# Token diffusion with earlier queries and squares, four single-bank PSUM tiles, two score tiles, and three more pauses in the work beside it

## Chip, cores and metric

The kernel runs on one core of one Trainium2 chip. The metric is the time on the device in microseconds. A profile of one execution accompanies the times; durations and waits come from it. The engines are TensorE (PE, with its weight loads PEld), VectorE (DVE), ScalarE (ACT), GpSimd (POOL) and SyncE (SP), which here issues most DMA transfers.

## What is computed

The reference chains four blocks on a tensor x of 8 sequences of 512 tokens and 256 channels: differential attention, two layers of local attention with a gated feed-forward part, a block of token and channel diffusion, and a mixture of 8 experts of which each token takes 2. Each block has the form x = x + layernorm(block(layernorm(x))). The change lies in the third block and in the beginning of the fourth:

```python
# token diffusion, 16 heads of 16 channels; queries and keys are the same projection
qk = (x @ Wqk).reshape(b, n, H, dh).transpose(0, 2, 1, 3)
v  = (x @ Wv).reshape(b, n, H, dh).transpose(0, 2, 1, 3)
dot = einsum('bhnd,bhmd->bhnm', qk, qk)
q2 = sum(qk * qk, axis=-1)
logits = (2.0 * dot - q2[..., :, None] - q2[..., None, :]) / sqrt(dh) * tau
out = einsum('bhnm,bhmd->bhnd', softmax(logits), v)
return out @ Wo            # reshaped back to (b, n, d)
# channel diffusion: the same between channels, 8 groups of 32
# x = x + token(ln(x)) * gamma1 ; x = x + channel(ln(x)) * gamma2
# experts, gate only:
gates = softmax(xf @ gate_w); topw, topi = top_k(gates, 2)
```

## The kernel before

All of x stays in SBUF as fp32. The kernel goes through the blocks one after the other. The third block (`diffusion`, which calls `tokens`) takes the eight sequences in turn; the experts follow when all are gated.

**Steps and slots.** `tokens` handles a sequence in four steps of four heads each; step n is sequence n // 4, heads 4 (n % 4) and up. Each step has four slots, k = 0 to 3, one for each tile of 128 tokens. The loop over `s` in `tokens` walks over all slots: `scores(n, k)` makes a group of four score products, one for each head in its own quarter of TensorE's rows, into two PSUM tiles `tsa` of two heads each, and ACT turns each into exponentials `te` (L1007, L1011). `sums` multiplies the exponentials with the values into one accumulator `tpo` for the step (L1020), which ACT copies to `toc`; `divide` transposes it (`tpt`), and DVE divides by the sum of the exponentials (L1039, L1040: `trec`, `to`). 

**Queries and squares.** `queries(n + 1)` projects the next step's queries and keys (`tqk`). ACT copies the product to `tkT` (L955), DVE squares it (`tsq`, L956), POOL scales it to `tqT` (L957). `squares(n + 1)` sums the squares with a product (`tq`) and adds them to `tkT` and `tqT` on DVE (L965, L968). Only then can the scores of step n + 1 begin. In this kernel queries stand in slot k = 1 and squares in slot k = 2. (All `tau` are positive in the inputs, so the branch `known` is the one that runs.)

**Work beside it.** Two queues of generators, `between` and `ahead`, are advanced from the loop: a call runs one generator as far as its next `yield`. `between` is called twice in every slot. It holds `finish(b)` of the sequence before, 17 calls, and then `gate(b)`, 10 calls. `finish` transposes the output (`toT`, copied by ACT and DVE in turn), multiplies it by Wo (`pp`), normalises (`th`), does the channel diffusion (`cqk`, `cpd`, `cpr`, `cpw`, `cpv`, and a `pp` with the folded weight `wvc`), and adds the result to x on POOL (L889). `gate` takes moments of x, normalises it into `xf`, stores it, transposes it, makes the gate's product `pg`, ranks the eight experts for each token on DVE and POOL (`ahead`, `same`, `rank`, `sel`, `run`), makes the positions with two products into `ppos`, and scatters the rows of `xf` to DRAM with eight indirect DMAs from POOL (L1228). `xf` has a single buffer, so the next gate's first write to it (L1169, on POOL) waits until those have landed. `ahead` holds `prepare(b + 1)`: norms, transposes and values of the next sequence.

**PSUM.** There are eight banks. Pool `t_big` has three tiles of two banks for scores; pool `t_ps` has two tiles of one bank for everything else: `tqk`, `tq`, `tpo`, `tpt`, and all the products of finish, gate and prepare.

**Order.** The order of the instructions on each engine is set when the program is built: a planner takes the instructions in the order of the text, with its own costs, and lets those marked `high_priority(offset=HOLD)` go ahead. Groups marked `keep_in_program_order` stay together. On the chip each engine runs its own list in order, and a semaphore wait holds all that stands behind it.

Of the kernel before, what the change touches and what calls it, by code (L numbers as in the profile page):

```python
# [14 lines left out]
PSUM = bass.MemoryType.PSUM  # L15
# [101 lines left out]
class Net:  # L117
# [690 lines left out]
    def diffusion(self, nb, rest):  # L808

        nc, g = self.nc, self.dw
        later = lambda n, b, **k: rest.enter_context(self.tc.tile_pool(name=n, bufs=b, side="right", **k))
        wk, small, ps = later("t_wk", 1), later("t_small", 3), later("t_ps", 2, space=PSUM)
        tiles = lambda x: [x[:, t, :] for t in range(NT)]
        last = (wk.tile([P, NT, D], F32, name="tyl", tag="tyl"), wk.tile([P, NT, TH, 16], F32, name="tol", tag="tol"))

        def finish(b, y, o):

            oT = wk.tile([P, DC, S], F32, name="toT", tag="chT")  # L820
            self.turned(ps, o.rearrange("p t h e -> p t (h e)"), oT)
            yield

            def add(t0, pp):
                nc.vector.tensor_add(y[:, t0:t0 + 2, :], y[:, t0:t0 + 2, :], pp)

            for t0 in range(0, NT, 2):
                self.project(ps, lambda t: [oT[:, c, self.tok(t)] for c in range(DC)], [g["o"][:, c, :] for c in range(DC)], add, [t0])
                yield

            made = self.moments(small, tiles(y))
            yield
            h = wk.tile([P, NT, D], F32, name="th", tag="th")
            self.normed(tiles(y), tiles(h), *made)
            yield
            hT = wk.tile([P, DC, S], F32, name="chT", tag="chT")
            self.turned(ps, h, hT, g["g2"], g["b2"])
            yield
            qk = wk.tile([P, NT, D], F32, name="cqk", tag="cqk", bufs=1)
            for t0 in range(0, NT, 2):  # L840
                self.project(ps, lambda t: [hT[:, c, self.tok(t)] for c in range(DC)], [g["cqk"][:, c, :] for c in range(DC)],
                             lambda t0, pp: self.copy(qk[:, t0:t0 + 2, :], pp), [t0])
                yield
            pd = ps.tile([P, DC, P], F32, name="cpd", tag="ps")
            for i in range(DC):
                self.mm(pd[:, i, :], [(qk[:, t, self.tok(i)], qk[:, t, self.tok(i)]) for t in range(NT)])
            dot = small.tile([P, DC, P], F32, name="dot", tag="dot", bufs=1)
            nc.vector.tensor_copy(dot, pd)
            dg = small.tile([P, DC, P], F32, name="dg", tag="dg", bufs=1)
            nc.vector.tensor_mul(dg, dot, self.ident.unsqueeze(1).to_broadcast([P, DC, P]))  # L850
            yield
            pr = ps.tile([P, DC, P], F32, name="cpr", tag="ps")
            self.mm(pr, [(self.const[:, C_ONE:C_ONE + P], dg)])

            nc.vector.scalar_tensor_tensor(dot, dot, 2.0, pr, ALU.mult, ALU.subtract)
            for i in range(DC):
                nc.vector.scalar_tensor_tensor(dot[:, i, :], dot[:, i, :], g["ct"][:, i:i + 1],
                                               self.const[:, C_BLK:C_BLK + P], ALU.mult, ALU.add)
            nm = small.tile([P, DC], F32, name="cnm", tag="cnm")
            nc.vector.tensor_reduce(nm, dot, AX.X, ALU.max, negate=True)  # L860
            rs = small.tile([P, DC], F32, name="crs", tag="crs")
            for i in range(DC):
                nc.scalar.activation(dot[:, i, :], dot[:, i, :], AF.Exp, bias=nm[:, i:i + 1], accum_out=rs[:, i:i + 1])
            nc.vector.reciprocal(rs, rs)
            nc.vector.tensor_mul(dot, dot, rs.unsqueeze(2).to_broadcast([P, DC, P]))
            yield
            yield

            pw = ps.tile([P, DC, D], F32, name="cpw", tag="ps")
            for i in range(DC):  # L870
                self.mm(pw[:, i, :], [(dot[:, i, :], g["co"][:, i, :])])
            wc = wk.tile([P, DC, D], F32, name="wc", tag="wc", bufs=1)
            self.copy(wc, pw)
            yield
            pv = ps.tile([P, DC, D], F32, name="cpv", tag="ps")
            for i in range(DC):
                self.mm(pv[:, i, :], [(g["cv"][:, c, self.tok(i)], wc[:, c, :]) for c in range(DC)])
            wv = wk.tile([P, DC, D], F32, name="wvc", tag="wvc", bufs=1)
            self.copy(wv, pv)
            yield  # L880
            yield
            for t0 in range(0, NT, 2):
                if t0:
                    yield
                self.project(ps, lambda t: [hT[:, c, self.tok(t)] for c in range(DC)], [wv[:, c, :] for c in range(DC)], add, [t0])
            made = self.moments(small, tiles(y))
            yield
            self.normed(tiles(y), tiles(y), *made)
            nc.gpsimd.tensor_add(self.xb(b), self.xb(b), y)  # L889
            self.between.add(self.gate(b, wk, small, ps))  # L890

        self.logs = True
        flag = nc.values_load(self.flag, min_val=0, max_val=1)
        with self.tc.If(flag > 0) as known:
            self.tokens(nb, True, wk, small, ps, finish, last)
        with known.Else():
            self.tokens(nb, False, wk, small, ps, finish, last)
        self.joint()
        self.between = Between()
        self.between.add(finish(nb - 1, *last))  # L900

    def joint(self):
# [3 lines left out]
    def tokens(self, nb, known, wk, small, ps, finish, last):  # L906
# [4 lines left out]

        with ExitStack() as ctx:
            pool = lambda n, b, **k: ctx.enter_context(self.tc.tile_pool(name=n, bufs=b, **k))
            step, big = pool("t_step", 2), pool("t_big", 3, space=PSUM)
            nc, g = self.nc, self.dw
            state, qk, es, pos, outs = {}, {}, {}, {}, {}
            group = lambda i: slice(32 * i, 32 * i + 32)
# [42 lines left out]
            def squares(n):  # L960
                qT, kT, sq = qk[n]
                pq = ps.tile([P, S], F32, name="tq2", tag="ps")
                self.mm(pq, [(self.const[:, C_G:C_G + P], sq)])
                with self.tc.high_priority(offset=HOLD if known else 0):
                    nc.vector.scalar_tensor_tensor(kT, pq, self.const[:, C_K17:C_K17 + 1], kT, ALU.mult, ALU.add)  # L965
                    if known:
                        r = n % 4
                        nc.vector.scalar_tensor_tensor(qT, pq, g["sq"][:, r:r + 1], qT, ALU.mult, ALU.add)  # L968
# [76 lines left out]
            total = 4 * nb  # L1045
# [6 lines left out]
            for s in range(4 * (total + 1) if known else 0):  # L1052
                n, k = divmod(s, 4)
                if n < total:
                    scores(n, k)
                if k == 0 and n:
                    sums(n - 1, 2)
                    sums(n - 1, 3)
                if k == 1 and n + 1 < total:
                    queries(n + 1)  # L1060
                if k == 1 and n:
                    divide(n - 1)
                if k == 2 and n + 1 < total:
                    squares(n + 1)
                if k == 3 and n < total:
                    sums(n, 0)
                    sums(n, 1)
                if k == 1 and n % 4 == 0 and n < total:
                    if n // 4 + 1 < nb:
                        ahead.add(prepare(n // 4 + 1))  # L1070
                    if n:
                        b = n // 4 - 1
                        between.add(finish(b, state[b][0], outs.pop(("o", b))))
                between()
                if k % 2:
                    ahead()
                between()
            for s in range(0 if known else 8 * (total + 2)):
                n, j = divmod(s, 8)
# [77 lines left out]
    def gate(self, b, wk, small, ps):  # L1157
# [33 lines left out]
        nc.vector.tensor_tensor(same, theirs, mine, ALU.is_equal)  # L1191
        nc.gpsimd.tensor_mul(same, same, tie.unsqueeze(1).to_broadcast([P, NT, NE, NE]))
        nc.gpsimd.tensor_add(ahead, ahead, same)
        rank = small.tile([P, NT, NE], F32, name="rank", tag="rank")
        nc.vector.tensor_reduce(rank, ahead, AX.X, ALU.add)
        yield
# [7 lines left out]
            nc.vector.memset(run[:, 0, :], 0.0)  # L1204
        for t in range(NT):
            nc.vector.tensor_add(run[:, t + 1, :], run[:, t, :], sel[:, t, :])
        pp = ps.tile([P, NT, NE], F32, name="ppos", tag="ps")
        flat = lambda x: x.rearrange("p t e -> p (t e)")
        self.mm(flat(pp), [(row(C_TRI, P), flat(sel)), (row(C_ONE, P), flat(run[:, 0:NT, :]))])
# [261 lines left out]
```

## Time and profile before

| | us |
|---|---|
| median of 3 runs | 4023.95 (4018.45 to 4028.95) |
| the profiled execution | 4028.8 |
| its span | 4027.1 |
| PE busy | 3577.5 |
| DVE busy | 2220.8 |
| ACT busy | 1828.2 |
| POOL busy | 1612.7 |
| score products of token diffusion, first to last start | 2778.5 to 3443.9 |

The span is the time from the first to the last recorded instruction. An engine's busy time is a share of that span, and neither tells by itself what the end waits for. A timeline row gives an instruction's start, its duration, and in brackets how long its engine stood idle before it and whose end released it. A granted clock of 1.00 is TensorE's full speed.

### The profile page before, as it was taken

Reading aid. Unit: us, or ns where it says so; the run is one execution under the profiler, and the core shown is the slowest. Engines: PE = TensorE matmul, PEld = TensorE weight load, DVE = VectorE, ACT = ScalarE, POOL = GpSimd, SP = SyncE. Lnnn points to the kernel's source line nnn. Section 1 sums busy time; section 2 is a strip of 40 time slices with the busy share of each in tenths; the row PEclk is TensorE's granted clock in tenths of the full one; section 3 lists DMA queues with packets and bytes.
Section 4 is the critical chain, followed back from the end, with each engine's and each line's share of the span. In section 5 each row is a group of like instructions: output and inputs, shape, how many; then the busy total and the mean of one; then the engine's idle time right before and its main releaser. Section 6 shows DMA issues by size and latency. Waiting matters only on the chain. (4 is left out here: it accounts for less than half of the span.)

```text
span 4027.1 us, 53567 instructions
## 1 busy us (share of the span) xinstructions
PE 3577.5 (89%) x20002; PEld 1911.0 (47%) x20002; DVE 2220.8 (55%) x4380; ACT 1828.2 (45%) x3639; POOL 1612.7 (40%) x1459
## 2 busy tenths in 40 slices
PE   8999999999878999999999999977888888578883
PEld 3343434443335555555555555643444444355562
DVE  6677767776636666665555555533444433344444
ACT  3555555555524444444444444424555444223333
POOL 3666666666644333333333333311111111143344
PEclk8999999999979999999999999988999999789996
DMA  9200000000000000000000000000000000421123
GB/s 349 98 1 6 6 6 1 6 6 6 6 32 1 5 4 3 3 23 4 9 29 9 9 9 9 9 16 22 16 17 16 16 16 16 145 66 53 52 89 104
DMA packets 92878, 130.46 MB, mean 32 GB/s; under 512 B 23040, under 2 KB 71238, under 8 KB 92614
## 3 DMA queue, kind: packets, MB, share of 16 engines
q1 hardware_dynamic: 86086, 109.10, 8.3%
q0 software_dynamic: 6528, 17.87, 1.2%
q8 instruction: 162, 2.65, 0.3%
q14 instruction: 102, 0.84, 0.1%
HBM read 57.58 MB, written 65.18 MB: 30 GB/s over the span
## 5 line engine op out<-in xcount | busy, mean ns | idle before, releaser
L359 ACT ACTIVATE e<-sa 128x1024 f32<-128x1024 f32 (+3 forms) x512 | 359.2, 702 | 347.8 <-PE sa L352 345.3
L380 POOL TENSOR_TENSOR e<-e,e 128x1536 f32<-128x1536 f32 (+2 forms) x192 | 451.6, 2352 | 98.7 <-PE po L375 88.7
L352 PE MATMUL sa<-qT,kT 32*128 32x512 f32 (+3 forms) x2048 | 436.6, 503 | 8.5 <-ACT e L359 8.1
L342 PE MATMUL sc<-kT,qT 32*128 32x128 f32 (+3 forms) x2048 | 427.5, 499 | 8.7 <-DVE spread L356 5.2
L356 DVE TENSOR_REDUCE spread<-sc 128x2 f32<-128x256 f32 (+3 forms) x512 | 422.1, 825 | 15.3
L633 ACT ACTIVATE lp<-lp,lnm 128x256 f32<-128x256 f32 (+1 forms) x512 | 240.0, 470 | 255.8 <-DVE lnm L625 161.1
L200 PE MATMUL lpa<-ghT,lw 128*128 128x512 f32 (+1 forms) x768 | 341.5, 599 | 14.7 <-ACT ghT L546 14.7
L637 POOL TENSOR_TENSOR lp<-lp,lrs 128x1024 f32<-128x1024 f32 x64 | 121.1, 1893 | 550.5 <-DVE lrs L634 550.5
L355 DVE TENSOR_TENSOR sc<-sc,const 128x256 f32<-128x256 f32 x512 | 218.5, 427 | 166.6 <-PE sa L352 142.6
L342 PEld LDWEIGHTS sc<-kT,qT 32*128 32x128 f32 x2048 | 161.9, 190 | 287.6 <-issue 126.1
L1011 ACT ACTIVATE te<-tsa 128x1024 f32<-128x1024 f32 x256 | 250.4, 1023 | 71.1 <-PE tsa L1007 59.9
L200 PE MATMUL lqk<-qkv,lhT 128*128 128x512 f32 x512 | 246.0, 619 | 2.3 <-DVE qk L584 1.6
L585 POOL TENSOR_TENSOR qk<-qk,over 128x1024 f32<-128x1024 f32 x64 | 151.2, 2363 | 216.1 <-DVE qk L584 216.1
L200 PEld LDWEIGHTS lpa<-ghT,lw 128*128 128x128 f32 (+1 forms) x768 | 133.0, 178 | 207.8 <-issue 167.6
L362 POOL TENSOR_SCALAR_AFFINE_SELECT e<-e 128x512 f32<-128x512 f32 x256 | 160.3, 639 | 172.6 <-ACT e L359 172.5
L1324 ACT ACTIVATE ehT<-eht,enorm 128x128 f32<-128x128 f32 x288 | 108.0, 457 | 232.0 <-PE eht L1320 232.0
L375 PE MATMUL po<-e,v 128*32 128x512 f32 (+3 forms) x2048 | 189.9, 454 | 4.0 <-POOL e L362 3.6
L200 PE MATMUL lpp<-lw,u 128*128 128x256 f32 (+1 forms) x768 | 193.2, 396 | 0.0
L622 DVE TENSOR_TENSOR lp<-lsc,const 128x768 f32<-128x768 f32 (+1 forms) x128 | 138.6, 1083 | 91.6 <-PE lsc L619 91.5
L619 PE MATMUL lsc<-lkT,lqT 64*128 64x256 f32 (+1 forms) x1024 | 158.1, 388 | 27.6 <-DVE qk L584 27.6
L352 PEld LDWEIGHTS sa<-qT,kT 32*128 32x128 f32 x2048 | 161.1, 191 | 42.9 <-ACT e L359 26.7
L200 PE MATMUL py<-ew,ehT 128*128 x576 | 146.6, 399 | 37.5 <-ACT ehT L1324 19.4
(277 smaller groups left out, 6865.8 us busy)
## 6 DMA issues: line engine op xcount, KB each, us to landing
xrows<-zero SPq DMA_DIRECT2D x66, 514.0 KB
ex<-xrows SPq DMA_DIRECT2D x72, 128.5 KB
ew<-in_L_ffn_w_dram SPq DMA_DIRECT2D x16, 512.0 KB
egot<-yrows SPq DMA_DIRECT2D x16, 512.0 KB
x<-in_L_attn_X_dram SPq DMA_DIRECT2D x8, 512.0 KB
saved<-x SPq DMA_DIRECT2D x8, 512.0 KB
lx<-saved SPq DMA_DIRECT2D x8, 512.0 KB
xf<-xf SPq DMA_DIRECT2D x8, 512.0 KB
```

The costliest lines, as they stand in the source:

```text
L200: self.nc.tensor.matmul(out, lhsT=l, rhs=r, start=i == 0, stop=i == len(pairs) - 1)
L342: nc.tensor.matmul(sc[:, i, :w], lhsT=qT[g, self.tok(t)], rhs=kT[g, :w], start=True, stop=True)
L352: nc.tensor.matmul(sa[:, i, :S - k * P], lhsT=kT[g, self.tok(k)], rhs=qT[g, k * P:], start=True, stop=True)
L355: nc.vector.tensor_add(sc[:, :, w - P:w], sc[:, :, w - P:w], own)
L356: nc.vector.tensor_reduce(self.spread[n % 2][:, t, g0:g0 + 2, 0 if n % 2 else 16], sc[:, :, :w], AX.X, ALU.max, negate=True)
L359: nc.scalar.activation(x[:, h0:h0 + 2, :], sa[:, :, :S - k * P], AF.Exp, scale=0.25)
L362: nc.gpsimd.affine_select(x[:, :, :P], x[:, :, :P], [[0, 4], [1, P]], ALU.is_ge, 0.0, base=0, channel_multiplier=-1)
L375: nc.tensor.matmul(pos[n][group(g), k * P:], lhsT=seqs[b][1][:, k, 4 * r + g, :], rhs=x[:, g, :], start=k == 0, stop=k == 2)
L380: nc.gpsimd.tensor_add(y, y, es.pop((n, k)))
L619: nc.tensor.matmul(sc[:, i, c0:c0 + m * P], lhsT=qT[r, h, self.tok(t)], rhs=kT[r, h, k0 * P:(k0 + m) * P], start=True, stop=True)
L633: nc.scalar.activation(x, x, AF.Exp, bias=nm[:, i, k:k + 1], accum_out=rs[:, i, k:k + 1])
L1011: nc.scalar.activation(e[:, 2 * i:2 * i + 2, :], sa[i], AF.Exp)
```

## The change

Four things change, all in the third block and in the gate:

- `queries` of the next step move from slot k = 1 to slot k = 0, and `squares` from slot k = 2 to slot k = 1.
- Pool `t_ps` gets four banks instead of two.
- Pool `t_big` gets two score tiles instead of three. All eight banks are in use as before.
- Three more `yield`s are put in: one in `finish` between the add to x and the moment at which the gate joins the queue, one in `gate` ahead of the rank, one ahead of the product for the positions.

```diff
-        wk, small, ps = later("t_wk", 1), later("t_small", 3), later("t_ps", 2, space=PSUM)
+        wk, small, ps = later("t_wk", 1), later("t_small", 3), later("t_ps", 4, space=PSUM)
...
             nc.gpsimd.tensor_add(self.xb(b), self.xb(b), y)
+            yield
             self.between.add(self.gate(b, wk, small, ps))
...
-            step, big = pool("t_step", 2), pool("t_big", 3, space=PSUM)
+            step, big = pool("t_step", 2), pool("t_big", 2, space=PSUM)
...
-                if k == 1 and n + 1 < total:
+                if k == 0 and n + 1 < total:
                     queries(n + 1)
                 if k == 1 and n:
                     divide(n - 1)
-                if k == 2 and n + 1 < total:
+                if k == 1 and n + 1 < total:
                     squares(n + 1)
...
         nc.gpsimd.tensor_add(ahead, ahead, same)
+        yield
         rank = small.tile([P, NT, NE], F32, name="rank", tag="rank")
...
             nc.vector.tensor_add(run[:, t + 1, :], run[:, t, :], sel[:, t, :])
+        yield
         pp = ps.tile([P, NT, NE], F32, name="ppos", tag="ps")
```

The line numbers in the text are those of the kernel before; in the changed kernel lines behind the first `yield` move down by one, behind the second by two and behind the third by three.

## The prediction, made before the changed kernel was run

> **What bounds the kernel now.** I read the page, then busy time and clock by stretch, then TensorE's own timeline, then who ended its idle time. The page gives the whole:
>
> ```profile
> PE 3577.5 (89%) x20002; PEld 1911.0 (47%) x20002; DVE 2220.8 (55%) x4380; ACT 1828.2 (45%) x3639; POOL 1612.7 (40%) x1459
> PEclk8999999999979999999999999988999999789996
> ```
>
> TensorE (PE) is the busiest engine, and the edits lie only in token diffusion, 2778 to 3450 us of the span. Busy time and granted clock, first of three long stretches of that stage, then of one sequence cut at TensorE's holes:
>
> ```profile
> 2778.00:2858.00 80.00, 78.09 (x469) 31.88 (x468) 23.64 (x57) 54.50 (x68) 7.08 (x6) 1.00 0.00 1
> 2858.00:3396.00 538.00, 474.32 (x2653) 231.12 (x2654) 221.05 (x679) 274.07 (x393) 97.61 (x103) 0.93 0.05 18
> 3149.53:3153.47 3.94, 0.00 (x1) 0.03 (x1) 2.26 (x7) 0.28 (x1) 2.40 (x2) 0.82 0.00 0
> 3153.47:3158.50 5.03, 5.03 (x14) 1.71 (x14) 3.32 (x17) 4.50 (x8) 0.00 (x0) 0.50 0.21 73
> 3169.49:3172.33 2.84, 0.00 (x0) 0.03 (x1) 1.19 (x7) 1.94 (x2) 1.36 (x2) 1.00 0.00 0
> 3172.33:3179.66 7.33, 7.18 (x20) 3.31 (x20) 3.28 (x17) 0.69 (x1) 3.92 (x5) 0.53 0.15 54
> ```
>
> Columns: length, then PE, weight loads, DVE, ACT, POOL, the clock, DMA. The first sequence has no finish or gate of another beside it and nearly no holes (78.09 of 80). Then six sequences take 538 us, 89.7 each (cpd product to cpd product, 2857.86 to 3395.86). Two holes recur in each, 3.94 and 2.84 us, and after each the clock is half (0.50, 0.53) for 5.03 and 7.33 us: 2.5 + 3.4 = 5.9 us lost besides. Who ended TensorE's holes, 2862 to 3450:
>
> ```profile
> PE pt L192 <- DVE to L1040: 23.6, 6, 3.9
> PE ppos L200 <- DVE two L1217: 14.2, 5, 2.8
> PE tsa L1007 <- DVE tqT L968: 12.0, 7, 1.7
> PE cpw L200 <- DVE dot L865: 5.3, 7, 0.8
> PE pt L192 <- ACT chT L196: 2.9, 5, 0.6
> ```
>
> So a sequence loses 3.94 + 2.84 + 1.72 + 0.75, about 1.1 in small ones (0.26, 0.23, 0.58), and 5.9 of clock: 16.2 of 89.7 us. What is left is work: a group of four score products takes 1.07 us start to start, two value groups (tpo) 1.86, tqk 1.75, tq 0.96, tpt 0.53, a pp of eight products 3.6, eight transposes 1.05.
>
> **What the change removes, from the order in which the changed program is built.**
> - The 3.94: a transpose (pt) waits for the bank that tpt holds until DVE's `to`, and DVE stands in order behind bn_stats of x, which waits 2.35 us for POOL's add (L889). Four banks free it, and the gate's moments now come after tpt's readers. -3.94.
> - The 2.84: ppos waits for the ranking on DVE and POOL (3168.4 to 3172.3). With the new yields there stand, between pg and ppos, scores 1.07, tpt 0.53, tq 0.96, four pp 1.83 and scores 1.07: 5.5 us against a chain of some 5 (tsq 0.7 now in it). -2.84.
> - The 1.72: scores wait for tqT (L968), as tq came one slot earlier than they. Two slots lie between now. -1.72.
> - The half clock behind the first two: -5.9.
> Sum -14.4 us a sequence. Joined transposes give some -0.4.
>
> **What it adds.** The built order is fixed per engine, so I walked it with the durations above.
>
> A. *The scatter.* In before, three scatter DMAs, POOL's tqT (L957), then five; the tqT after those came late enough to wait for nothing:
>
> ```profile
> 3178.57 0.88 POOL L957 TENSOR_SCALAR tqT<-tkT,dsa,dsb 128x512 f32<-128x512 f32 x1
> 3179.62 1.02 POOL L1228 DMA_INDIRECT xrows<-xf,slots  x1 [0.17 <-issue]
> ...
> 3184.73 0.96 POOL L1228 DMA_INDIRECT xrows<-xf,slots  x1 [0.30 <-issue]
> 3187.66 0.54 POOL L1169 TENSOR_SCALAR xf<-const 128x4 f32<-128x4 f32 x2 [1.97 <-DMA xrows<-xf,slots]
> 3192.41 1.26 POOL L957 TENSOR_SCALAR tqT<-tkT,dsa,dsb 128x512 f32<-128x512 f32 x1 [4.22 <-ACT tkT L955]
> ```
>
> After the change all eight DMAs stand together, then the next gate's token column (it waits until they have landed), then tqT of the next sequence's second step, whose queries come earlier. From ppos: slots 3.1 us, first issue 3.4, eight issues at 1.26 (five took 6.07) to 13.25, landing 2 to 2.5, column 0.54, tqT 1.0: 17 us. DVE then does tqT's square (L968, 0.74) and only behind it the copy of toT (0.69), which pp of Wo needs: 18.7. TensorE gets there after ppos 1.04, scores 2.0, tpo 1.86, scores 1.07, tpo 1.86, tqk 1.75, scores 1.07, tpt 0.53, tq 1.0, pt 1.05, scores 1.07: 14.3. It stands 4.4 us, and the half clock after it costs 2.7 (between 2.5 and 3.4). +7.1.
>
> B. *Two tiles of scores.* A group's first pair waits for the first exponential of the group before, its second pair for the second. ACT reads in order:
>
> ```profile
> 3153.97 0.30 ACT L156 ACTIVATE rs<-mv,const 128x4 f32<-128x4 f32 x1 [4.16 <-DVE mv L173]
> 3154.30 0.21 ACT L157 ACTIVATE rs<-rs 128x4 f32<-128x4 f32 x1
> 3154.41 1.00 ACT L1011 ACTIVATE te<-tsa 128x1024 f32<-128x1024 f32 x1
> ```
>
> There an exponential stands behind the gate's rs, that one behind bn_stats of x and POOL's add. It still does. From the end of pp of Wvc: ty 1.8, rs, normalised by 4.6, add to 7.0, four bn_stats and aggregates to 8.9, rs to 9.5, exponential to 10.5. Now the last score group of that step needs it, and stands directly behind the third: TensorE arrives at 5.1, waits 1.4 for the first exponential, works 0.86, waits 3.1, works 0.86. That and 0.45 in the group before is 5.7 us more than the work, and 2.7 of half clock. +8.4.
>
> C. Other split groups: beside ppos 0.9, around cpr 1.4 (the exponentials of one group, 1.94 us, against 0.54 of cpr between). +2.3.
>
> D. th: both rs now stand together on ACT behind both sets of moments, and transposes wait about 2.0 where 1.07 was lost. +1.0 (0 to 2).
>
> Added 18.8 against 14.8 removed: +4.0 us for each of seven sequences, +28. In the first sequence, where before has next to no holes, third and fourth score group are adjacent in each of four steps; a pair at 2.2 and one at 3.2 us after the group's start instead of 1.07 ends about 1.5 later: +6. The gate's extra yields use 30 of 32 calls of the queue, so nothing spills into the next sequence; the tail's waits (3445 to 3520) are its own dependency chain, 0. No instruction is added.
>
> Sum: profiled span 4027.1 + 34 = 4061; the execution took 4028.8, the median of the runs is 4023.95, so **4058 us**.
>
> **A rule against the row.** Half clock is the term I know least. Row: half clock followed a hole of 2.84 us as well as one of 3.94. The Trainium skill, "TensorE: Matmul & The Clock Gate", section "HAM oscillation — how this bites in real kernels", has only idle gaps longer than about 3.4 us matter. By the rule B's holes (1.4, 3.1) would cost no clock, and the 2.84 removed should not have: 7 x 2.7 = 19 us less, 4039. By the row, 4058. I keep the row, measured in this stage, and put the rule's value in the range.
>
> **Rivals.**
> 1. *Faster, 0.20.* A isn't there. Place: pp of Wo, once a sequence. Price: 7.1 x 7 = 50 us, so 4008; with the clock rule also 3989. It decides when POOL's chain from ppos to tqT is shorter than TensorE's way there, 14.3 us instead of 18.7: if under about 0.5 us of A's 7.1 is left, the sum is below -12. For it: both holes named by the profile do go. Against: eight issues at 1.26 and a landing of 2 us are read from before.
> 2. *The exponentials pace everything, 0.17.* ACT was busy 46 us of 89; with every group tied to the one before, each late copy on ACT (toc, tkT) also holds TensorE. Split groups at some twelve more places cost 0.86 each: 10 us x 8, 4140. Against: most groups have 2.5 us or more of other products between.
> 3. *Banks and clock pay each other off, 0.12.* Half clock in A and B is smaller (38 us less): 4020, no change.
>
> **How the numbers follow.** My case 0.51. 0.3% of this time, 12 us, is about what can be told from no change. Its own range is 4025 to 4090 (4 us a sequence either way). The range for 8 in 10 reaches into rivals 1 and 2: 3988 to 4112. My case has 0.03 of its chance within 0.3%: faster 0.20, same 0.15, slower 0.65.
>
> **What would show it.** Right: no hole at pt behind `to`, none over 1 us at ppos; a hole of 3 to 5 us before pp of Wo, released by DVE toT, and POOL's tqT ending about 17 us after ppos; a hole of about 3 us inside a score group, released by ACT te; a sequence of 93 to 95 us; first sequence about 6 us longer. Wrong: sequences under 89 us, clock above 0.95 in this stage, or POOL's tqT free before the squares.

## The result, and the profile after

The changed kernel takes 4048.33 us (median, 4038.52 to 4057.56) against 4021.39 us before (4016.55 to 4032.38), measured side by side: a ratio of 1.006, interval 1.0043 to 1.0078. That is slower by 27 us; 4058 was predicted. The profiled execution of the changed kernel took 4039.01 us, one of its fastest, and that of the kernel before, at 4028.8, lies in the upper half of its runs. So the two traces differ by 10 us only, and what follows explains the stage in which the edits lie, not each of the 27.

The page of the changed kernel, TensorE's share and its granted clock:

```profile
PE 3601.6 (89%) x20002; PEld 1914.0 (47%) x20002; DVE 2222.8 (55%) x4380; ACT 1830.5 (45%) x3639; POOL 1612.4 (40%) x1459
PEclk8999999999979999999999999988989999789996
```

No instruction was added, and TensorE is busy for 24 us longer. Busy time by stretch, with the columns of the prediction (length, then PE, weight loads, DVE, ACT, POOL, the clock, DMA), for the first sequence and the six behind it, cut at the first cpd product of each:

```profile
2778.00:2862.94 84.94, 79.60 (x452) 31.88 (x453) 22.36 (x53) 53.42 (x66) 6.74 (x6) 1.00 0.00 1
2862.94:3411.87 548.93, 494.14 (x2653) 232.96 (x2652) 222.56 (x679) 274.44 (x393) 96.72 (x102) 0.92 0.05 18
```

Six sequences take 548.9 us, 91.5 each, where they took 538.0 (89.7). TensorE idles less (54.8 us for 63.7) and is busy longer (494.1 for 474.3). Who ended its idle time, 2862 to 3450 us of the changed kernel (total, times, longest):

```profile
PE tsa L1008 <- ACT te L1012: 32.4, 27, 3.5
PE pp L200 <- DVE toT L149: 17.5, 6, 4.7
PE cpw L200 <- DVE dot L865: 5.3, 7, 0.8
PE pt L192 <- DVE th L181: 4.9, 6, 0.9
```

All three rows that led this list before (pt behind `to`, ppos, scores behind tqT) are gone. Two new ones stand for them: scores behind an exponential (the prediction's B) and the product with Wo behind `toT` (its A). TensorE's timeline in the first of the six sequences has both, in the bracket of the row:

```profile
2891.30 1.13 PE L1008 MATMUL tsa<-tqT,tkT 32*128 32x512 f32 x4 [1.13 <-ACT te L1012]
2895.18 2.08 PE L1008 MATMUL tsa<-tqT,tkT 32*128 32x512 f32 x4 [2.76 <-ACT te L1012]
...
2935.45 6.32 PE L200 MATMUL pp<-dwo,toT 128*128 128x256 f32 x14 [4.71 <-DVE toT L149]
```

For B, ScalarE's timeline of the same sequence shows who is late:

```profile
2893.68 0.30 ACT L156 ACTIVATE rs<-mv,const 128x4 f32<-128x4 f32 x1 [2.44 <-DVE mv L173]
2894.01 0.20 ACT L157 ACTIVATE rs<-rs 128x4 f32<-128x4 f32 x1
2894.12 1.01 ACT L1012 ACTIVATE te<-tsa 128x1024 f32<-128x1024 f32 x1
```

The exponential has its scores, but stands behind the gate's `rs`, for which ScalarE waits 2.44 us. For A, GpSimd's timeline and then VectorE's (ppos was at 2915.60):

```profile
2928.12 0.96 POOL L1231 DMA_INDIRECT xrows<-xf,slots  x1 [0.30 <-issue]
2931.95 0.53 POOL L1170 TENSOR_SCALAR xf<-const 128x4 f32<-128x4 f32 x2 [2.87 <-DMA xrows<-xf,slots]
2932.59 0.77 POOL L958 TENSOR_SCALAR tqT<-tkT,dsa,dsb 128x512 f32<-128x512 f32 x1
```

```profile
2933.39 0.75 DVE L966 SCALAR_TENSOR_TENSOR tkT<-tq,const,tkT 128x512 f32<-128x512 f32 x1 [5.43 <-POOL tqT L958]
2934.06 0.74 DVE L969 SCALAR_TENSOR_TENSOR tqT<-tq,dsq,tqT 128x512 f32<-128x512 f32 x1
2934.72 0.68 DVE L149 COPY toT<-pt 128x512 f32<-128x512 f32 x1
```

The last of eight scatter DMAs, the token column that waits for their landing, tqT at last (it ends 17.8 us after ppos), VectorE's two squares behind 5.43 us of waiting, and `toT` behind those.

**A ledger of the six sequences.** From the records of TensorE and of its clock over the six sequences of a trace I added up the time without PE work ("idle"), the clock that was not granted (1 less the clock, times the length: "half clock"), the part of it that fell on busy time, and the rest of PE's busy time ("work at full clock", in which score products that stand in pairs instead of fours are included with their longer time):

| us in six sequences | length | idle | half clock | of it on busy time | work at full clock |
|---|---|---|---|---|---|
| before | 538.0 | 63.7 | 35.8 | 31.3 | 443.0 |
| after | 548.9 | 54.8 | 42.7 | 36.8 | 457.4 |

So the change won 8.9 us of holes and gave back 5.4 of clock and 14.4 of work. The holes removed were larger than those made; the loss is where no row of waits shows it. Taken by tile, the work has grown at the score products: 125.0 us at full clock where they took 105.3, while all other products together take 5.3 less.

### The profile page after: what moved, and what is told of

It reads as the page before. It is cut to its first block, busy times and chain, and to the rows that moved or that the text cites. A ratio compares the mean times of both kernels' runs of the same rounds, so it can differ in the third digit from the quotient of the medians.

```text
span 4037.3 us, 53548 instructions
## 1 busy us (share of the span) xinstructions
PE 3601.6 (89%) x20002; PEld 1914.0 (47%) x20002; DVE 2222.8 (55%) x4380; ACT 1830.5 (45%) x3639; POOL 1612.4 (40%) x1459
## 5 line engine op out<-in xcount | busy, mean ns | idle before, releaser
L1008 PE MATMUL tsa<-tqT,tkT 32*128 32x512 f32 x1024 | 187.0, 660 | 38.1 <-ACT te L1012 38.0
L958 POOL TENSOR_SCALAR tqT<-tkT,dsa,dsb 128x512 f32<-128x512 f32 x32 | 34.6, 1081 | 459.2 <-ACT tkT L956 458.6
```

What stands on the lines that cost most here:

```text
L1008: m = nc.tensor.matmul(sa[i // 2][:, i % 2, :], lhsT=kT[q, self.tok(k)], rhs=qT[q, :], start=True, stop=True)
```

## Experiments

Each is compared with runs of the kernel before on the same chip. "Period" is the mean of the six sequences in its own trace. The kernel before has 89.7, the changed one 91.5.

| run | what it is | median us | ratio to before | interval | period us |
|---|---|---|---|---|---|
| e1_psum | before + bank split | 4055.32 | 1.0058 | 1.0037 to 1.0078 | 92.8 |
| e1_queries | before + moved queries and squares | 4025.62 | 0.9988 | 0.9979 to 0.9997 | 88.7 |
| e1_yields | before + three pauses | 4030.35 | 1.0003 | 0.9992 to 1.0013 | 91.0 |
| e1_qy | after, bank split undone | 4059.68 | 1.0066 | 1.0042 to 1.009 | 95.5 |
| e2_qact | after, tqT on ScalarE | 4014.66 | 0.9974 | 0.9963 to 0.9986 | 85.6 |
| e2_rspool | after, gate's rs on GpSimd | 4016.28 | 0.9982 | 0.9971 to 0.9993 | 87.0 |
| e2_both | after, with both | 3990.88 | 0.9914 | 0.9891 to 0.9936 | 82.1 |
| e2_before_qact | before, tqT on ScalarE | 4022.82 | 0.9996 | 0.9985 to 1.0008 | 89.7 |
| e3_sums | e2_both, first value product earlier | 4012.01 | 0.9958 | 0.9944 to 0.9973 | 86.4 |
| e3_three_tiles | e2_qact, bank split undone | 4018.05 | 0.9973 | 0.9964 to 0.9982 | 89.5 |
| e3_no_pauses | e2_both without the pauses | 4008.71 | 0.9947 | 0.9931 to 0.9964 | 85.6 |
| e4_no_queries | e2_both without the moved queries | 4049.47 | 1.0053 | 1.0039 to 1.0068 | 91.4 |

The period is not the whole of a run: the first and the last sequence change too, and what stands behind the seventh cpd product takes 620 to 638 us in the fourteen traces. In e1_yields, for one, the six sequences are 8 us longer than before and the stretch from the seventh to the eighth cpd product is 7 shorter (70.8 for 77.7).

**The parts alone.** Each of the first three has only its own lines of the change's diff; e1_qy has all but the two lines of the pools:

```diff
-        wk, small, ps = later("t_wk", 1), later("t_small", 3), later("t_ps", 4, space=PSUM)
+        wk, small, ps = later("t_wk", 1), later("t_small", 3), later("t_ps", 2, space=PSUM)
...
-            step, big = pool("t_step", 2), pool("t_big", 2, space=PSUM)
+            step, big = pool("t_step", 2), pool("t_big", 3, space=PSUM)
```

> Only the PSUM split of the change (four small banks, two score tiles); queries, squares and pauses as before. Theory (the sum of the prediction): the hole at pt behind DVE to (3.94 us) goes, with 2.5 of half clock; the hole at ppos (2.84) stays; hole A stays away, as POOL's scatter order is that of before; the hole inside a score group (B, 1.1 + 2.8 us in the changed kernel) is there, with its half clock, and the first sequence is about 5 us longer. Net about +1 to +3 us a sequence: 4030 to 4050. Rival (the two score tiles cost nothing for themselves, the loss is in the queries and the scatter): the 6.4 us a sequence are won, about 3980, and the first sequence is no longer than before.

> Only the move of queries and squares by one slot; banks, score tiles and pauses as before. Theory: the wait of scores for tqT (1.7 us a sequence) goes, the holes at pt (3.9) and ppos (2.8) stay, no hole inside a score group; 4010 to 4025. Rival (the earlier queries by themselves put tqT behind the gate's work on POOL and make hole A): slower, 4030 to 4050, with a wait at pp of Wo behind DVE toT.

> Only the three pauses; banks, score tiles, queries and squares as before. Theory: the hole at ppos (2.8 us) goes with its half clock (3.4), and the gate's moments leave DVE before to, so that the hole at pt shrinks as well; nothing of A or B is there: 3970 to 4000. Rival (the pauses only move the wait, for what runs on TensorE's spare time anyway): within 12 us of before, 4010 to 4034.

> The whole change without the PSUM split (two small banks, three score tiles). Theory: B and the split score groups are gone, the first sequence is as before, hole A (pp of Wo behind DVE toT, mean 2.9 us in the changed kernel) is still there: 5 to 8 us a sequence less than the changed kernel, 3985 to 4010. Rival (half clock comes whatever the holes are, so that the score tiles are not what costs): within 12 us of the changed kernel, 4036 to 4060.

The bank split alone costs 0.58%, as much as the whole change, a little above the range given; its first waits, 2862 to 3450:

```profile
PE tq L200 <- DVE tsq L956: 21.0, 7, 3.2
PE tsa L1007 <- DVE tqT L968: 19.6, 6, 3.6
PE tsa L1007 <- ACT te L1011: 12.6, 20, 1.5
PE ppos L200 <- DVE two L1217: 5.0, 5, 1.0
```

The hole at pt behind `to` is gone, but not its cause. VectorE still stands behind the moments of x; now `tsq` is caught there too, and the squares' product waits 3 us for it. The 2.8 us hole of B did not come (the longest wait for an exponential is 1.5), and tqT waits for the scatter here as well: at 3013.6 it stands behind all eight DMAs. So the mechanisms that I expected of this kernel were the wrong ones, though the time was nearly right.

The moved queries alone are 0.12% faster, below what can be told from no change, as expected. What I did not expect is the row for pt behind `to`: 6.6 us in all where it was 23.6. With the queries a slot earlier VectorE does tqk's and tpt's work ahead of the moments. The holes shrink from 63.7 to 45.8 us in six sequences, but half clock grows from 35.8 to 39.2 and work by 9.

The three pauses alone change nothing (the rival). The hole at ppos is away, without a row; in its place stand smaller ones, and the hole at pt was not touched, against what I expected:

```profile
PE pt L192 <- DVE to L1041: 23.7, 6, 3.9
PE tsa L1008 <- DVE tqT L969: 12.0, 7, 1.7
PE tpo L1021 <- DVE tqT L969: 5.7, 5, 1.1
```

Without the bank split the change is as slow (1.0066), where 3985 to 4010 was expected. The hole of the scatter became larger, since with two small banks the transposes of `to`, ahead of the product with Wo, already wait for the bank that the squares hold until VectorE has used tqT. First rows of its waits:

```profile
PE pt L192 <- DVE tqT L969: 36.8, 12, 6.3
PE pp L200 <- DVE to L1041: 13.4, 6, 2.2
```

So "the bank split is the loss and the rest is a gain" is wrong. Nor does A belong to one of the edits. GpSimd's timeline of e1_queries, behind the eighth scatter DMA:

```profile
2920.81 0.54 POOL L1169 TENSOR_SCALAR xf<-const 128x4 f32<-128x4 f32 x2 [2.40 <-DMA xrows<-xf,slots]
2921.45 1.11 POOL L957 TENSOR_SCALAR tqT<-tkT,dsa,dsb 128x512 f32<-128x512 f32 x1
```

In e1_psum (3013.6), e1_yields (2929.95) and e1_qy (2930.42), too, a tqT stands behind all eight, where in the kernel before only three were ahead of it. What differs is which product of TensorE needs that tqT, and how soon: scores in e1_psum, transposes for up to 6.3 us in e1_qy, the product with Wo in the whole change. B needs the two score tiles and the new order together, since neither e1_psum nor e1_qy has such a hole. So there are no two halves of this change of which one could be kept, and the next experiments take A and B away and leave the change whole.

**A and B taken away.** e2_qact scales tqT on ScalarE; e2_rspool computes the gate's `rs` on GpSimd, which the kernel does elsewhere; e2_both has both; e2_before_qact is the first edit in the kernel before:

```diff
-                    nc.gpsimd.tensor_scalar(qT, kT, g["sa"][:, r:r + 1], g["sb"][:, r:r + 1], ALU.mult, ALU.add)
+                    nc.scalar.activation(qT, kT, AF.Identity, bias=g["sb"][:, r:r + 1], scale=g["sa"][:, r:r + 1])
...
+        logs, self.logs = self.logs, False
         made = self.moments(small, tiles(self.xb(b)))
+        self.logs = logs
```

> The changed kernel with tqT scaled by ACT instead of POOL (32 instructions of about 0.7 us move to ACT, which has room), so that the scatter DMAs on POOL no longer stand before it. Theory (A is POOL's scatter ahead of tqT): the holes at pp of Wo behind DVE toT (17.5 us in six sequences) and the half clock beside them go: 15 to 40 us less than the changed kernel, 4008 to 4033. Rival (what holds toT is DVE's own queue, or the half clock comes anyway): within 12 us of the changed kernel.

> The changed kernel with the gate's rs (4 values a partition) computed on POOL instead of ACT, so that no exponential stands behind it. Theory (B is the exponential behind rs): the holes of 2.76 us inside a score group go, with the half clock behind them: 15 to 40 us less than the changed kernel, 4008 to 4033; A stays as it is or grows by what TensorE comes earlier. Rival (two score tiles make it wait for the exponential whatever stands ahead on ACT): within 12 us of the changed kernel, the same holes released by ACT te.

> The changed kernel with both: tqT on ACT and the gate's rs on POOL. Theory: A and B are all that the change adds beside split score groups, so their sum is won: 35 to 75 us less than the changed kernel, 3973 to 4013, faster than before. Rival (the two hide each other, as a hole later in the same stretch takes up what the first leaves): no more than the better of the two alone.

> The kernel before with tqT on ACT, as the control: there tqT waits for no scatter that TensorE feels. Theory: only the part of the wait of scores for tqT (1.7 us a sequence) that POOL's 0.9 to 1.3 us made is won: 4010 to 4030, no change that counts. Rival (POOL's tqT is what paces all versions): 20 us or more faster than before.

Each repair turns the slower kernel into one faster than before: 1.006 to 0.9974 (34 us by the medians) and to 0.9982 (32 us). Together they give 0.9914, 57 us less than the changed kernel, most of 34 + 32. The waits, 2862 to 3450, first of e2_qact:

```profile
PE tsa L1008 <- ACT te L1012: 33.9, 28, 2.8
PE cpw L200 <- DVE dot L865: 5.3, 7, 0.8
PE pt L192 <- DVE th L181: 5.1, 6, 0.9
```

of e2_rspool:

```profile
PE tsa L1008 <- ACT te L1012: 15.9, 27, 1.1
PE pp L200 <- DVE toT L149: 12.8, 6, 3.1
```

of e2_both, with its six sequences below:

```profile
PE tsa L1008 <- ACT te L1012: 15.6, 25, 1.1
PE cpw L200 <- DVE dot L865: 8.6, 8, 3.3
```

```profile
2870.38:3362.83 492.45, 468.52 (x2653) 225.62 (x2652) 220.93 (x679) 289.70 (x405) 79.58 (x90) 0.98 0.06 20
```

Each edit removes its own row and leaves the other's: `toT` falls from 17.5 to 0.3 us with tqT on ScalarE (a row of 0.3 is left), the longest wait for an exponential from 3.5 to 1.1 with `rs` off ScalarE. A and B are thus shown as causes. In the kernel before, tqT on ScalarE is worth nothing, so ScalarE is not simply the better place for it. The same control was not run for `rs`; in the trace of the kernel before TensorE waits for exponentials for 0.3 us in all between 2862 and 3450, so little could be won there by this path. The ledger:

| us in six sequences | length | idle | half clock | of it on busy time | work at full clock |
|---|---|---|---|---|---|
| e2_qact | 513.4 | 39.2 | 22.2 | 17.9 | 456.3 |
| e2_rspool | 522.1 | 37.0 | 25.6 | 25.5 | 459.5 |
| e2_both | 492.4 | 23.9 | 10.2 | 10.2 | 458.3 |

Taking A away won 15.6 us of holes and 18.9 of clock: more than half of its price was clock. The work stays at 456 to 460 in all three, 13 to 16 above before, and again at the score products (125 to 127 us at full clock, 105.3 before). That part of the change's cost is neither A nor B. The prediction has split score groups (C) for it; the next runs bear on that.

**Can C go too, and is each part needed?** e3_sums is e2_both with one value product a slot earlier, so that it stands between two score groups:

```diff
-                if k == 3 and n < total:
+                if k == 2 and n < total:
                     sums(n, 0)
+                if k == 3 and n < total:
                     sums(n, 1)
```

e3_three_tiles is e2_qact with two small banks and three score tiles (`rs` stays on ScalarE). e3_no_pauses and e4_no_queries are e2_both without the three `yield`s, and with queries and squares in slots 1 and 2.

> The changed kernel with tqT on ACT, the gate's rs on POOL, and besides the first value products of a step (sums of tile 0) in slot 2 instead of slot 3, so that four groups of eight value products stand apart between score groups instead of two pairs. In the built order 28 of the 128 score groups of this stage then become 3 that have less than 0.87 us of other work ahead of them. Theory (C, groups split by the exponential of the group before, each 0.5 to 1.1 us of hole and 0.86 of half-filled array): 25 groups by 1.0 to 1.6 us are won, 25 to 40 us less than with both: 3950 to 3966. Rival (the split groups only wait for what TensorE waits for later anyway): within 12 us of both, 3979 to 4003.

> The moved queries, the three pauses and tqT on ACT, with the banks of the kernel before (two small, three score tiles). Theory (with two small banks a transpose waits for the bank that tq or tpt holds, whatever makes tqT): the holes of 5.8 us behind tqT at the scatter go, those behind to and thT stay, 3990 to 4015, so the four banks are worth something beside B. Rival (the three score tiles are worth as much as the four banks): 3975 to 3990, as good as the changed kernel with both repairs.

> The changed kernel with both repairs (tqT on ACT, the gate's rs on POOL) but without the three pauses. Theory: the hole at ppos (about 1.0 to 2.8 us with its half clock of 2.5) comes back in six or seven sequences, 10 to 35 us more than with both: 4000 to 4025. Rival (the pauses do nothing once A and B are gone): within 12 us of both, 3979 to 4003.

> The changed kernel with both repairs (tqT on ACT, the gate's rs on POOL) but with queries and squares in the slots of the kernel before. Theory (the sum of the prediction: the move of queries takes away the wait of scores for tqT, 1.72 us a sequence, with up to 3.4 of clock): that wait is back, 10 to 35 us more than with both: 4000 to 4025. Rival (a later square stands between score groups that are adjacent in the changed kernel, 12 short gaps instead of 28 among the 128 score groups, and that is worth more than the wait): as fast as both or faster, 3965 to 3995.

e3_sums missed by far: 4012.01, some 18 us slower by the ratios than e2_both instead of 25 to 40 faster. Its waits for exponentials do fall (12.2 us, 8 times, in place of 15.6, 25 times), but the score products were busy for 140.9 us of the six sequences, where they were for 132.6 in e2_both and 119.0 before. Eight value products take 0.93 us: with a group's 1.07 that makes 2.0 between two groups, against 1.94 of ScalarE for one group's exponentials. The gap is filled to the edge and not past it. The score products' own work did not fall: at full clock they take 127.1 us, as in e2_both (127.0), and the 8 us by which they were busy longer are half clock. Over the six sequences e3_sums has 11.6 us more of idle time than e2_both, 10.3 more of clock and 4.3 more of work; its largest new row is transposes behind `to` (8.3 us, 4 times). The ScalarE timeline where TensorE waits 1.98 us, before a score group that starts at 3071.20:

```profile
3068.44 1.05 ACT L1179 COPY xf<-xf 128x1024 f32<-128x1024 f32 x1 [4.45 <-DVE xf L181]
3069.70 0.30 ACT L156 ACTIVATE rs<-mv,const 128x4 f32<-128x4 f32 x1 [0.22 <-DVE mv L173]
3070.03 0.20 ACT L157 ACTIVATE rs<-rs 128x4 f32<-128x4 f32 x1
3070.14 1.92 ACT L1012 ACTIVATE te<-tsa 128x1024 f32<-128x1024 f32 x2
```

The exponentials stand behind the gate's copy of xf and another `rs`: B again, one place further on. I take that as the cause of this 2 us; what brought the other holes and their clock was not tested.

e3_three_tiles gives 0.9973 beside 0.9974 of e2_qact: once A is gone, the four banks with two score tiles and the two with three come to the same, as long as `rs` stays on ScalarE. The holes at the scatter are gone there too, as expected. Whether three tiles with both repairs would do as well as e2_both was not tried. The score products take 115.5 us at full clock in this run, 9.7 less than in e2_qact and still 10.2 more than before. So the two score tiles make about half of what the score products gained, and the transposes (33.4 us for 26.1) give most of that back; queries and pauses alone add 4.7 and 5.8 without a change of tiles, by a cause that stays open. "Split by two tiles" is thus only part of C.

Without the pauses e2_both, the fastest of these kernels, loses 18 us by the medians, 13 by the ratios (4008.71, within the range given), but not by the mechanism expected: only 1.1 us of waits stand at ppos. Its idle time is 30.3 us against 23.9, and half clock 32.4 against 10.2.

Without the moved queries it loses 58 us by the medians, 56 by the ratios, where 35 was the most expected. The waits and VectorE's timeline:

```profile
PE tsa L1008 <- ACT te L1012: 23.6, 20, 4.0
PE tq L200 <- DVE tsq L957: 21.1, 7, 3.2
```

```profile
3078.92 0.75 DVE L171 BATCH_NORM_STATS2 st<-x 128x6 f32<-128x256 f32 x2 [2.47 <-POOL x L889]
3079.59 0.67 DVE L957 TENSOR_TENSOR tsq<-tkT 128x512 f32<-128x512 f32 x1
3080.18 0.25 DVE L1040 RECIPROCAL trec<-tpt 128x16 f32<-128x16 f32 x1
```

`tsq` is ready for a long time and stands behind bn_stats of x, which waits 2.47 us for GpSimd's add. It is the stall of the kernel before, that held `to` there and holds `tsq` now; half clock is 47.8 us.

## Why the prediction was right, and by which of its steps

The direction was right, and the size: 4058 was predicted, 4048 measured, inside the likeliest case's own range (4025 to 4090). The owners of the new waits, A and B, were right as well, and the runs that take them away show it. The balance behind the number was not, and that the number came so near is in part luck. The sum, sorted by the columns of the ledger:

| us a sequence, change | holes | clock on busy time | work | sum |
|---|---|---|---|---|
| predicted | +3.7 (-8.5, then 4.4 in A, 4.5 in B, 2.3 in C, 1.0 in D) | -0.5 | +0.8 (1.2 in B, less 0.4) | +4.0 |
| measured | -1.5 | +0.9 | +2.4 | +1.8 |

The new holes were to outweigh the old ones; they did not. Clock and work made the kernel slower, by 3.0 us a sequence more than they had in the sum, and this paid for part of the 5.2 by which the holes were put too high. The steps in turn:

- **Removed, 3.94, 2.84 and 1.72.** All three holes are gone. The owners were named wrongly in two places. The 3.94 was put down to the four banks and the place of the moments, and only the 1.72 to the moved queries. Alone, the banks turned the 3.94 into 3.0 at `tq`; it is the earlier queries that take `tsq` and `to` out from behind the moments (23.6 to 6.6 us alone; 58 us in e4_no_queries). The 2.84 at ppos was put down to the pauses alone. With them alone it has no row, but they are not needed for it: e3_no_pauses has 1.1 us at ppos over all sequences. Since the sum was made for the whole change, neither slip harmed it.
- **Removed, 5.9 of half clock; added, 2.7 in A and 2.7 in B.** -0.5 a sequence in the sum, and +1.1 in the ledger (42.7 less 35.8, over six; 0.9 of it on busy time), so the sign was wrong. The clock was charged one price for each hole, and it doesn't go by single holes (last section).
- **A, hole 4.4 + 2.7 clock.** The mechanism is as described: POOL's tqT ends 17.8 us after ppos (17 predicted), and `toT` is what releases TensorE. The hole was 4.71, 1.59, 3.12, 1.76, 3.35 and 2.97 us, 2.9 in the mean against 4.4. (That TensorE came later where it had lost time to half clock before would account for the smaller ones; it was not tested.) The whole price, by e2_qact, is 91.5 - 85.6 = 5.9 a sequence (7.1 predicted).
- **B, holes 1.4 + 3.1.** 1.13 and 2.76 in the first sequences, at the places named, released by ACT te behind the gate's `rs`. Taking `rs` away removes the second with its clock: 4.5 a sequence, where 3.1 + 2.7 was predicted for it. All waits for exponentials come to 27.9 us in the six sequences, 4.7 each, where B and C together had 6.8.
- **C and B's split work.** C's 2.3 are waits; the longer work of split groups stands in the sum with 1.2 only, in B. The work at full clock grew by 14.4 in six, 2.4 a sequence, and that of the score products by 3.3. This is the term that the sum left nearly out, and e3_sums denies that spreading the value products cures it.
- **D, 1.0.** Transposes wait 0.8 to 0.9 for th once a sequence, where 2.0 was predicted and 1.07 was lost in small holes before. These are gone, so D added nothing.
- **First sequence, +6.** From the first score product to the first cpd 86.70 us against 79.40: +7.3, by five splits of 0.6 to 1.2 us at ACT te.
- **The sum.** The six sequences and the first should have been 30 us longer; in the profiled execution they are 18. The last stretch, from the seventh cpd product to the eighth, was to lose 4 and did not change (77.5 for 77.7). A sequence takes 91.5 us, where 93 to 95 was named as a sign of being right.
- **The rule against the row.** The row was the better one: half clock came with holes far shorter than 3.4 us (1.13 and 2.76; 0.48 and 0.76). But neither prices a hole.

The rivals: the first, "A isn't there", is false of the changed kernel, but e2_qact made it true, and 4014.66 was measured where the rival's sum was 4008. The second, exponentials that pace everything, is not what happened: te held TensorE for 32 us of waits, of which e2_rspool removed half without an exponential the less. The third, banks and clock paying each other off, is nearest to being the other truth: +1.8 a sequence is less than half of what I forecast, though the clock did not get smaller, as it assumed.

One gap stays. The trace puts the profiled execution 10 us behind that of before, the medians 27. The stage is 16 us behind at the seventh cpd product (3411.87 against 3395.86) and some of that is made up behind it; single executions of the changed kernel lie 19 us apart. No trace of a slower execution exists to say where those lost more.

## What to carry to other kernels

A wait that is taken away from one instruction stays on its engine for whatever stands next in order: before sizing a change, list for each engine what is queued behind the instruction that waits (here GpSimd behind the scatter, ScalarE behind four numbers of `rs`, VectorE behind bn_stats). Two short pieces of work (tqT, 0.77 to 1.27 us each time on GpSimd, and the gate's `rs`, 0.5 us each time on ScalarE) moved to engines without that queue turned a loss of 0.6% into a gain of 0.9% over the kernel before, while no single part of the change gained more than 0.12% by itself. And add up clock and work beside the holes: a change may reduce idle time and still be slower.

## What the runs showed of the hardware

Half clock comes in pieces of one length. Three windows around such stretches in the changed kernel (length first, the clock third from the end):

```profile
2870.00:2874.00 4.00, 4.00 (x14) 1.46 (x14) 0.00 (x0) 1.47 (x2) 0.00 (x0) 0.58 0.00 0
2934.00:2942.00 8.00, 6.55 (x18) 4.86 (x22) 3.42 (x9) 0.00 (x0) 0.00 (x0) 0.57 0.00 0
2986.00:2997.00 11.00, 8.47 (x28) 2.80 (x29) 5.23 (x23) 4.69 (x8) 0.00 (x0) 0.54 0.14 49
```

Lost are 0.42 x 4 = 1.7, 0.43 x 8 = 3.4 and 0.46 x 11 = 5.1 us: one, two and three times 1.7, that is, half clock for 3.4, 6.8 and 10.2 us. The sums of the six sequences are whole multiples too: 35.8 before is 21 pieces of 1.706, 42.7 after is 25, 22.2 is 13, 25.6 is 15, and 10.2 in e2_both is 6. This agrees with the window of 3.4 us which the Trainium skill, "TensorE: Matmul & The Clock Gate", section "What's actually happening", describes; the price of a hole is thus a whole number of pieces, and the prediction's 2.7 lies between one and two.

Whether a piece starts goes with the idle time that falls into one window, not with the longest hole. The clock records of each of the fourteen traces have all starts of half clock on one grid of 3.413 us. I took TensorE's idle share in every window of this grid, 2776 to 3480 us, in all fourteen. Of the windows at full clock with under 30% idle 25 of 2195 were followed by half clock; with 30 to 55%, 102 of 182; with more, 120 of 121. A window at half clock with 15% or more idle was followed by another in 118 of 118 cases. This is a count over runs that differ in much else, and no run changed the idle time of a window by itself. The first of the three stretches above followed holes of 0.48 and 0.76 us, which fall into one window, 36% of it:

```profile
2867.07 2.04 PE L1008 MATMUL tsa<-tqT,tkT 32*128 32x512 f32 x8 [0.48 <-ACT te L1012]
2869.87 1.99 PE L200 MATMUL cpw<-dwco,dot 128*128 128x256 f32 x4 [0.76 <-DVE dot L865]
```

In the first sequence of the same kernel six holes of 0.6 to 1.2 us were followed by none; no window there had more than 34% idle. What decides between 30 and 55% is not settled. Products in a quarter of the rows, split groups and transposes lie near many of these stretches; no run here separates them from the idle time.
